# Loading the first weight products' operands by halves of their columns, and moving the rank rows of B behind four products

## The chip, the cores and the metric

The kernel runs on one NeuronCore of a Trainium2 chip. The metric is the device time of one execution in microseconds. A core has engines that run side by side, each with its own queue of instructions in order: TensorE (PE, matrix products), VectorE (DVE) and ScalarE (ACT) and GpSimd (POOL) for elementwise work, and SyncE (SP), which here only issues transfers from DRAM into SBUF, the memory on the chip. Products accumulate in banks of PSUM. Instructions of different engines wait for one another by semaphores.

## The reference

One block of a transformer on x (32 sequences of 64 tokens, 1024 features, float32):

```python
base  = einsum('bsi,oi->bso', x, W)                    # W: 1024 x 1024
low   = einsum('bsi,bir->bsr', x, lora_A[labels])      # rank 32
c     = base + einsum('bsr,or->bso', low, lora_B_w) * 0.5
qkv   = c @ w_qkv.T + b_qkv                            # 1024 q, 256 k, 256 v
...   # rotary positions, causal softmax attention, 32 heads over 8 key heads
x     = x + attention @ w_o.T + b_o
c2    = x @ W2.T + 2 * (rank-16 rows of two experts of eight)
x     = x + c2 @ W_base.T + b_base + 2 * (rank-16 rows of two experts of eight)
```

The kernel doesn't form c. It multiplies the weights first: W with w_qkv (called cq for the q columns and ckv for the rest), and W2 with W_base (cf). It keeps these products in DRAM (`cqkv`, `cffn`) and then applies them to x. The low-rank part goes the same way: the rows of `lora_B_w` times w_qkv are `b1q`, the "rank rows of B".

## The kernel before

**The weight products.** `multiply` (L514) forms a 1024 x 1024 product in four groups of two output blocks, each by a seven-product scheme (Strassen in Winograd's form; class `Group`, L220). Per group the left operand is a tile w of 256 outputs (128 partitions x 8 chunks x 256), of which `weight_sums` (L163) makes four sums s1 to s4 on GpSimd; the right operand is split by chunks (first and second H = 4 of 8) and by columns (first and second half), and `column_sums` (L176) makes four sums t1 to t4 of its quarters on VectorE. For cq the right operand is `wq`, 128 partitions x 8 chunks x 1024 columns. t1 (L182) is the second column half less the first, over the first four chunks; t2 (L184) takes t1 from the second column half of the last four chunks; t3 (L186) and t4 (L188) follow. One such sum is made per chunk, four each.

The seven steps of a group are p1 to p7 (L270 to L320). Each is four matrix products over the four chunks, eight instructions on TensorE, 128 x 512 outputs:

- p1 multiplies w's first four chunks, first 128 outputs, with wq's first four chunks, first column half. It fills bank x, tile cq_x in the profile.
- p2 adds to bank x the last four chunks of w, first 128 outputs, with wq's last four chunks, first column half.
- p6 multiplies s2 and t2 into bank y (cq_y); p5 multiplies s1 and t1 into bank z (cq_z); p7 adds s3 by t3 to bank y; p4 adds w's last quarter by t4 to bank y; p3 adds s4 by wq's last quarter to bank z. Between them VectorE and ScalarE read the banks, and ScalarE's queue writes the outputs to DRAM.

So p1 and p2 need one column half of wq and one output half of w alone; all the rest need sums over everything.

**The rank rows.** `rank_rows` (L473) multiplies b1 (1024 x 32 rows of B, 128 KB) with wq, four chunks at once in four stripes of 32 rows. It has two halves, `b1q_rows[0]` over wq's first four chunks and `b1q_rows[1]` over the last four, all columns, sixteen instructions each (tile b1q, L487). The second half copies two tiles on ScalarE and leaves a last step, two products `b1qs` (L480) that add the stripes, in the list `later`; `done_later` (L439) carries it out.

**The order.** TensorE's, VectorE's and SP's orders are written out by hand (`manual_schedule`, L120 to L125); GpSimd's and ScalarE's are left to a scheduler. For cq the first two groups are interleaved by the `order` list (L602): p1 of group 0, p1 of group 1, p2 of both, p6, p5, p7 of group 0, p6 of group 1, and so on. The dictionary `after` (L606) hangs other work behind a step: the first half of the rank rows behind (0, "p1"); `load_first` (L577) behind (0, "p2"), which carries out the second half of the rank rows and then issues the loads of x; `after_first_sum` (L589) behind (0, "p6"), which carries out `done_later`, makes t4, and prepares the gathers of `lora_A`.

**The loads.** SP issues them in the order of L551 to L560: w0 (group 0's w) first four chunks, wq's chunks 0 to 3 with b1 behind chunk 0, w1 first four chunks; then the same for the last four chunks; then `index` and the constants. Each chunk of wq is 512 KB in rows of 4 KB, and so is each half of w0 and w1. Eight loads of SP's queue are in flight at a time; the next one waits for the landing of the one eight before it. Group 2's w and then x wait for w0's last use, in (0, "p4").

Of the kernel before, what the change touches and what calls it, by code (L numbers as in the profile page):

```python
# [19 lines left out]
P = 128  # L20
D = 1024
KC = D // P
# [54 lines left out]
def block_kernel(ctx: ExitStack, tc: tile.TileContext, a, out: bass.AP):  # L77
    nc = tc.nc
# [33 lines left out]
    def load_x(hf):  # L112
        t = [xp.tile([P, TH], F32, tag=f"x{kc}", name=f"x{kc}_{hf}") for kc in range(KC)]
        for kc in range(KC):
            nc.sync.dma_start(t[kc], a["xT"][kc, :, hf * TH : (hf + 1) * TH])
        return t
# [17 lines left out]
    def labels_and_languages():  # L134

        nc.vector.tensor_copy(lab, index[:, :B])
        nc.vector.tensor_scalar(wrap, lab, 0.0, float(NL), ALU.is_lt, ALU.mult)
        nc.vector.tensor_add(lab, lab, wrap)
        nc.vector.tensor_scalar(lab, lab, 0.0, float(NL - 1), ALU.max, ALU.min)

        nc.vector.tensor_scalar(lab, lab, float(P), row, ALU.mult, ALU.add)
        nc.vector.tensor_copy(rows_of, lab)


        nc.vector.tensor_copy(lang, index[:, B:])
        nc.vector.tensor_scalar(lang, lang, float(E), None, ALU.subtract)
        nc.vector.tensor_tensor(
            lbias,
            em8.unsqueeze(1).to_broadcast([P, B // 2, E]),
            lang.unsqueeze(2).to_broadcast([P, B // 2, E]),  # L150
            ALU.is_equal,
        )
        nc.vector.tensor_scalar(lbias, lbias, 5.0, None, ALU.mult)
# [4 lines left out]
    H = KC // 2  # L158
# [274 lines left out]
    def new_low(hf):  # L433
        return hp.tile([P, TH], F32, tag="hw", name=f"low_{hf}")
# [4 lines left out]
    def done_later():  # L439
        while later:  # L440
            later.pop(0)()
# [15 lines left out]
    with tc.tile_pool(name="gen", bufs=1) as gen:  # L457
# [15 lines left out]
        def rank_rows(name, low, right, n, dst):  # L473


            banks = {at: ps_tile(f"{name}_{at}") for at in range(0, n, 512)}

            def stacked(at, rows):
                ps = ps_tile(f"{name}s_{at}")
                nc.tensor.matmul(ps, stack, rows, start=True, stop=True)  # L480
                nc.scalar.copy(dst[:, at : at + 512], ps)

            def half(i):
                for at, ps in banks.items():
                    for g in range(4):
                        kc = i * H + g
                        nc.tensor.matmul(  # L487
                            ps[g * LR : (g + 1) * LR], low[:, kc, :], right[:, kc, at : at + 512],
                            start=i == 0, stop=i == 1,
                        )  # L490
                    if i == 1:
                        rows = tmp(f"{name}o_{at}")
                        nc.scalar.copy(rows, ps)
                        later.append(lambda at=at, rows=rows: stacked(at, rows))

            return lambda: half(0), lambda: half(1)
# [48 lines left out]
        wq = gen.tile([P, KC, D], F32, tag="right", name="wq")  # L545
# [2 lines left out]
        w3x = gen.tile([P, KC, NF - D], F32, tag="w3x", name="w3x")  # L548
        b1 = gen.tile([P, KC, LR], F32, tag="b1", name="b1")
        w0, w1 = (wp.tile([P, KC, WG], F32, tag="w", name=f"w_cq{g}") for g in range(2))  # L550
        first_half, second_half = slice(0, H), slice(H, KC)  # L551
        for half in (first_half, second_half):
            nc.sync.dma_start(w0[:, half], a["w1"][0, :, half])
            for kc in range(half.start, half.stop):
                nc.sync.dma_start(wq[:, kc, :], a["wqkv"][:, kc, :D])
                if kc == 0:
                    nc.sync.dma_start(b1, a["b1"])
            nc.sync.dma_start(w1[:, half], a["w1"][1, :, half])
        nc.sync.dma_start(index, a["index"])
        nc.sync.dma_start(cst, a["consts"])  # L560
        b1q_rows = rank_rows("b1q", b1, wq, D, b1q)
# [9 lines left out]
        def gather_first(s):  # L571
            tags = iter(("w_os", "s_os"))
            first_pass[s] = gathered(
                0, s, lambda name: gen.tile([P, 4, KC * LR], F32, tag=next(tags), name=name), 4
            )

        def load_first(w):  # L577
            b1q_rows[1]()
            first_pass["x"], first_pass["low"] = load_x(0), new_low(0)

        def first_ranks(s):
            *halves_of_ranks, stacked = ranks(0, s, first_pass["x"], first_pass[s], first_pass["low"])
            for step in halves_of_ranks:
                step()
            later.append(stacked)
            if s == 0:
                gather_first(1)

        def after_first_sum(w):  # L589
            done_later()  # L590
            for kc in range(H):
                t_cq.make(kc, (3,))
            labels_and_languages()
            gather_first(0)

        def load_kv(w):
# [7 lines left out]
                *((0, "out11"), (0, "p4"), (0, "p3"), (1, "p5"), (1, "p7"), (1, "out11"), (1, "p4"), (1, "p3")),  # L604
            ],
            after={  # L606
                (0, "p1"): lambda w: b1q_rows[0](),
                (0, "p2"): load_first,
                (0, "p6"): after_first_sum,
                (1, "p3"): load_kv,  # L610
                (2, "p7"): lambda w: first_ranks(0),
                (2, "p4"): lambda w: done_later(),
# [137 lines left out]
    for hf in range(2):  # L750
# [264 lines left out]
        with tc.manual_schedule():  # L1015
# [3 lines left out]
            for u in range(2):  # L1019
                g = pair  # L1020
# [139 lines left out]
        w = wp.tile([P, KC, WG], F32, tag="w", name=f"w_h{hf}")  # L1160
# [165 lines left out]
```

## Time and profile before

| | us |
|---|---|
| median of 4 runs | 1227.49 (1226.78 to 1227.98) |
| profiled execution, its own time | 1226.07 |
| its span, first to last instruction | 1224.3 |
| TensorE busy | 1207.7 (99% of the span) |
| VectorE, GpSimd, ScalarE busy | 578.2, 512.2, 153.5 |
| first product starts | 7.27 |
| first landing of a load (half of w0) | 5.53 |
| landing of wq's chunk 4, and chunk 7 | 15.69, 19.55 |
| landing of w1's second half, the last of the weights | 20.81 |
| (0, "p6") starts, and the next product after it | 26.76, 30.20 |

The page gives busy times by engine, a chain of waits that ended last, and groups of instructions by line. Busy time of TensorE counts instructions that overlap as a pipeline, so 99% says that it is seldom without work, not that it runs at its peak. Idle time of another engine costs nothing as long as TensorE's chain doesn't pass through it. In rows that list instructions by time, the columns are start, length (both in us), engine, line, operation, what is written and read, and in brackets the idle time before and what ended it. "DMA" among the releasers is the landing of a load.

### The profile page before, as it was taken

Reading aid. Unit: us, or ns where it says so; the run is one execution under the profiler, and the core shown is the slowest. Engines: PE = TensorE matmul, PEld = TensorE weight load, DVE = VectorE, ACT = ScalarE, POOL = GpSimd, SP = SyncE. Lnnn points to the kernel's source line nnn. Section 1 sums busy time; section 2 is a strip of 40 time slices with the busy share of each in tenths; the row PEclk is TensorE's granted clock in tenths of the full one; section 3 lists DMA queues with packets and bytes.
Section 4 is the critical chain, followed back from the end, with each engine's and each line's share of the span. In section 5 each row is a group of like instructions: output and inputs, shape, how many; then the busy total and the mean of one; then the engine's idle time right before and its main releaser. Section 6 shows DMA issues by size and latency. Waiting matters only on the chain.

```text
span 1224.3 us, 13566 instructions
## 1 busy us (share of the span) xinstructions
PE 1207.7 (99%) x5434; PEld 610.8 (50%) x5434; DVE 578.2 (47%) x940; ACT 153.5 (13%) x282; POOL 512.2 (42%) x437
## 2 busy tenths in 40 slices
PE   7999999999999999999999999999999999999998
PEld 2444875555444477444444444444468444444443
DVE  4312141115557879753941113555879764743111
ACT  1001000000001124220000000001124330000000
POOL 3441361443434746843726111533646752822010
PEclk9999999999999999999999999999999999999999
DMA  6663732644111112023114234111111123212110
GB/s 240 211 212 108 270 123 82 206 148 146 35 34 35 36 70 70 17 67 126 35 35 138 69 122 153 35 35 35 35 70 33 39 70 98 76 35 69 48 56 35
DMA packets 57504, 108.83 MB, mean 89 GB/s; under 512 B 5088, under 2 KB 34144, under 8 KB 56160
## 3 DMA queue, kind: packets, MB, share of 16 engines
q1 hardware_dynamic: 41648, 79.53, 19.5%
q10 hardware_dynamic: 13104, 20.03, 4.5%
q0 software_dynamic: 2688, 8.39, 2.1%
q8 instruction: 43, 0.70, 0.3%
q14 instruction: 21, 0.17, 0.0%
HBM read 83.72 MB, written 24.22 MB: 88 GB/s over the span
## 4 chain that ended last, share of the span: by engine, by line
PE 94%; POOL 2%; DVE 2%; DMA 0%; issue 0%; ACT 0%; SPq 0%; POOLq 0%; DVEq 0%
PE qk_y L249 9%; PE f_y L249 7%; PE qk_x L249 6%; PE qk_z L249 6%; PE o_y L249 5%; PE v L843 5%; PE f_z L249 4%; PE f_x L249 4%; PE o_z L249 4%; PE o_x L249 4%; PE cq_y L249 3%; PE cf_y L249 3%; PE cq_x L249 2%; PE cq_z L249 2%; PE cf_x L249 2%; PE cf_z L249 2%
## 5 line engine op out<-in xcount | busy, mean ns | idle before, releaser
L793 POOL TENSOR_TENSOR raw<-raw,consts 128x512 f32<-128x512 f32 x40 | 65.4, 1646 | 99.8 <-DVE t L792 99.8
L897 POOL TENSOR_TENSOR e<-e,top 128x512 f32<-128x512 f32 x64 | 65.0, 1045 | 65.1 <-DVE top L896 50.1
L909 POOL TENSOR_TENSOR e<-e,tot 128x512 f32<-128x512 f32 x64 | 66.2, 1067 | 19.9 <-DVE tot L907 19.9
L249 PE MATMUL qk_x<-x,w_qk 128*128 128x512 f32 x160 | 72.9, 598 | 0.0
L249 PE MATMUL qk_y<-sum_x,s_qk 128*128 128x512 f32 x160 | 72.0, 593 | 0.0
L170 POOL TENSOR_TENSOR s_f<-w_f 128x512 f32<-128x512 f32 x8 | 11.2, 1403 | 121.1 <-DMA w_f<-cffn 99.6
L249 PE MATMUL o_x<-q,w_o 128*128 128x512 f32 x128 | 58.9, 592 | 0.0
L843 PE MATMUL v<-w_v,x 128*128 128x256 f32 x256 | 58.7, 382 | 0.0
L249 PE MATMUL f_x<-x,w_f 128*128 128x512 f32 x128 | 57.9, 592 | 0.0
L249 PE MATMUL f_y<-sum_y,s_f 128*128 128x512 f32 x128 | 57.5, 592 | 0.0
L906 DVE TENSOR_REDUCE tot<-e 128x8 f32<-128x512 f32 x64 | 40.2, 665 | 25.4 <-ACT e L901 25.1
L843 PEld LDWEIGHTS v<-w_v,x 128*128 128x128 f32 x256 | 47.4, 190 | 8.4 <-issue 2.6
L1001 POOL TENSOR_TENSOR x<-x,o_u 128x512 f32<-128x512 f32 x32 | 42.1, 1325 | 22.7 <-DVE o_u L291 18.4
L249 PEld LDWEIGHTS qk_x<-x,w_qk 128*128 128x128 f32 x160 | 29.6, 190 | 39.6 <-issue 39.6
L249 PEld LDWEIGHTS qk_y<-sum_x,s_qk 128*128 128x128 f32 x160 | 30.3, 190 | 37.9 <-issue 36.6
L170 POOL TENSOR_TENSOR s_qk<-w_qk 128x512 f32<-128x512 f32 x10 | 18.2, 1818 | 66.5 <-DMA w_qk<-cqkv 51.2
L794 DVE TENSOR_TENSOR t<-t,consts 128x512 f32<-128x512 f32 x40 | 45.0, 1137 | 1.0
L803 DVE TENSOR_TENSOR q<-raw,t 128x512 f32<-128x512 f32 x32 | 40.9, 1282 | 9.3 <-POOL raw L793 9.3
L901 ACT ACTIVATE e<-e 128x512 f32<-128x512 f32 x64 | 38.2, 640 | 47.4 <-POOL e L897 47.4
L887 DVE TENSOR_TENSOR e<-sc,consts 128x512 f32<-128x512 f32 x64 | 39.5, 679 | 8.1 <-PE sc L864 8.1
L249 PEld LDWEIGHTS f_x<-x,w_f 128*128 128x128 f32 x128 | 24.3, 190 | 30.6 <-issue 30.6
L249 PEld LDWEIGHTS f_y<-sum_y,s_f 128*128 128x128 f32 x128 | 24.3, 190 | 30.6 <-issue 30.6
(314 smaller groups left out, 2187.9 us busy)
## 6 DMA issues: line engine op xcount, KB each, us to landing
w_qk<-cqkv SPq DMA_DIRECT2D x10, 1024.0 KB, 5.6
x<-in_xT SPq DMA_DIRECT2D x16, 512.0 KB, 8.4
w_o<-in_wo SPq DMA_DIRECT2D x16, 512.0 KB, 4.8
s_o<-wos SPq DMA_DIRECT2D x16, 512.0 KB, 6.3
w_f<-cffn SPq DMA_DIRECT2D x8, 1024.0 KB, 5.6
outT<-o ACTq DMA_DIRECT2D x32, 256.0 KB, 2.4
wq<-in_wqkv SPq DMA_DIRECT2D x8, 512.0 KB, 9.0
cqkv<-cq ACTq DMA_DIRECT2D x16, 256.0 KB, 2.6
```

The lines of the kernel that those rows point to most:

```text
L170: nc.gpsimd.tensor_add(s[:, 0], a21, a22)
L249: nc.tensor.matmul(ps, self.weights[left][:, kc, :], self.right(right, kc), start=first and kc == 0, stop=kc == self.h - 1, skip_group_che ...
L793: nc.gpsimd.tensor_mul(rv, rv, c3)
L794: nc.vector.tensor_mul(t2v, t2v, s3)
L803: nc.vector.tensor_add(*unfinished.pop())
L843: nc.tensor.matmul(begun[t], x[kc][:, t * P : (t + 1) * P], wv[:, kc, :], start=False, stop=kc == KC - 1, skip_group_check=True,)
L887: nc.vector.tensor_add(per_key(e), per_key(sc), mask.unsqueeze(1).to_broadcast([P, 8, S]))
L897: nc.gpsimd.tensor_sub(ev, ev, wide(top))
L901: nc.scalar.activation(e, e, AF.Exp, scale=SCALE)
L906: nc.vector.tensor_reduce(tot[:, i], es[i], AX.X, ALU.add)
L909: nc.gpsimd.tensor_mul(es[i], es[i], wide(tot[:, i]))
L1001: nc.gpsimd.tensor_add(xo, xo, by_sequence(add))
```

## The change

The loads of w0, w1 and wq for the first weight products come in pieces. A chunk of wq is loaded in two halves of 512 columns, and a half of w0 or w1 in two pieces of 128 outputs. The pieces that p1 and p2 of the first two groups read go first: w0, wq and w1, first output half and first column half, for the first four chunks and then for the last four. Behind them come w0's second output half, b1, wq's second column half of chunks 0 to 3, w1's second output half, and wq's second column half of chunks 4 to 7. The bytes are the same. wq's rows in a load become 2 KB, those of w0 and w1 512 B; there are 25 loads in place of 13.

The first half of the rank rows moves from behind (0, "p1") to behind (1, "p2"), so that the four products p1, p1, p2, p2 run without it; the second half moves from `load_first`, behind (0, "p2"), to `after_first_sum`, behind (0, "p6"); and `done_later`, which stacks the stripes, moves from there to behind (0, "p3").

```diff
-        first_half, second_half = slice(0, H), slice(H, KC)
-        for half in (first_half, second_half):
-            nc.sync.dma_start(w0[:, half], a["w1"][0, :, half])
+
+        halves_of = slice(0, H), slice(H, KC)
+
+        def load_columns(kc, c):
+            cols = slice(c * D // 2, (c + 1) * D // 2)
+            nc.sync.dma_start(wq[:, kc, cols], a["wqkv"][:, kc, cols])
+
+        def load_outputs(w, g, half, r):
+            nc.sync.dma_start(w[:, half, r * P : (r + 1) * P], a["w1"][g, :, half, r * P : (r + 1) * P])
+
+        for half in halves_of:
+            load_outputs(w0, 0, half, 0)
             for kc in range(half.start, half.stop):
-                nc.sync.dma_start(wq[:, kc, :], a["wqkv"][:, kc, :D])
-                if kc == 0:
-                    nc.sync.dma_start(b1, a["b1"])
-            nc.sync.dma_start(w1[:, half], a["w1"][1, :, half])
+                load_columns(kc, 0)
+            load_outputs(w1, 1, half, 0)
+        for half in halves_of:
+            load_outputs(w0, 0, half, 1)
+        nc.sync.dma_start(b1, a["b1"])
+        for kc in range(H):
+            load_columns(kc, 1)
+        for half in halves_of:
+            load_outputs(w1, 1, half, 1)
+        for kc in range(H, KC):
+            load_columns(kc, 1)
         nc.sync.dma_start(index, a["index"])
         nc.sync.dma_start(cst, a["consts"])
...
         def load_first(w):
-            b1q_rows[1]()
             first_pass["x"], first_pass["low"] = load_x(0), new_low(0)
...
         def after_first_sum(w):
-            done_later()
+            b1q_rows[1]()
             for kc in range(H):
                 t_cq.make(kc, (3,))
...
             after={
-                (0, "p1"): lambda w: b1q_rows[0](),
                 (0, "p2"): load_first,
+                (1, "p2"): lambda w: b1q_rows[0](),
                 (0, "p6"): after_first_sum,
+                (0, "p3"): lambda w: done_later(),
```

## The prediction

> **What bounds the kernel now.** I read the page first, then the chain of waits for the stretch that the change touches (the first 62 us), then the order of time of VectorE, GpSimd and the DMA queue there, and last the transfer rates of loads with short rows.
>
> ```profile
> span 1224.3 us, 13566 instructions
> ...
> PE 1207.7 (99%) x5434; PEld 610.8 (50%) x5434; DVE 578.2 (47%) x940; ACT 153.5 (13%) x282; POOL 512.2 (42%) x437
> ...
> PE 94%; POOL 2%; DVE 2%; DMA 0%; issue 0%; ACT 0%; SPq 0%; POOLq 0%; DVEq 0%
> ```
>
> TensorE is the path nearly everywhere: 16.6 us of the span are not PE time, and 7.3 of them lie at the start. So the change can win only at the start, and loses what it adds there. The chain of waits for this stretch (start, length, what):
>
> ```profile
> 1.20 5.94 DMA wq<-in_wqkv
> ...
> 7.27 5.25 PE cq_x L249 x8
> 12.52 1.85 PE b1q L487 x16
> 14.38 7.06 PE cq_x L249 x16
> 21.44 1.85 PE b1q L487 x16
> 23.29 3.63 PE cq_x L249 x8
> 26.92 3.43 PE cq_y L249 x8
> 30.36 1.72 PE b1qs L480 x4
> ```
>
> The first product waits for the first 0.5 MB of weights w0 and the first 0.5 MB of wq, until 7.27. From there on TensorE waits for nothing: four products cq_x (p1, p1, p2, p2), the two halves of the rank rows b1q between them, and at 26.9 the first cq_y, p6. In order of time p6 begins at 26.76 and the next product at 30.20. A product of eight instructions takes 3.43 when its data are there. The first takes 5.25: its first four instructions start at 7.27, 8.26, 9.11 and 9.96, the last four 0.43 apart. wq's chunks 1 and 2 had landed by 8.78 and 10.05, so these starts are mostly a slower TensorE at its beginning, not data.
>
> p6 needs VectorE's second column sums (t2, L184), and these need the last columns of wq. VectorE and GpSimd in order of time:
>
> ```profile
> 15.79 1.75 DVE L184 TENSOR_TENSOR sum_cq<-wq,sum_cq 128x512 f32<-128x512 f32 x1 [7.93 <-DMA wq<-in_wqkv]
> 17.46 1.75 DVE L182 TENSOR_TENSOR sum_cq<-wq 128x512 f32<-128x512 f32 x1
> 20.81 0.68 DVE L182 TENSOR_TENSOR sum_cq<-wq 128x512 f32<-128x512 f32 x1
> 21.52 1.65 DVE L184 TENSOR_TENSOR sum_cq<-wq,sum_cq 128x512 f32<-128x512 f32 x1
> 24.88 1.64 DVE L184 TENSOR_TENSOR sum_cq<-wq,sum_cq 128x512 f32<-128x512 f32 x1
> ...
> 15.72 1.27 POOL L172 TENSOR_TENSOR s_cq<-w_cq 128x512 f32<-128x512 f32 x1
> 16.95 1.72 POOL L171 TENSOR_TENSOR s_cq<-s_cq,w_cq 128x512 f32<-128x512 f32 x1
> 20.88 1.75 POOL L170 TENSOR_TENSOR s_cq<-w_cq 128x512 f32<-128x512 f32 x1 [0.54 <-DMA w_cq<-in_w]
> ```
>
> Two readings. First, the same VectorE sum takes 0.68 while GpSimd waits for a load (20.81) and 1.65 to 1.75 while GpSimd adds weights; both engines then end one instruction every 1.67 (VectorE at 17.54, 19.2, 20.89): they take turns, 1.26 of GpSimd and about 0.4 of VectorE, and a sum ends 0.55 after the GpSimd instruction that it waited for. Second, the eighth sum ends at 26.52. p6 wants it only for its last chunk, 2.6 after its start at 26.76, so 2.8 of slack cover it. This slack, not TensorE's queue, is what the change spends.
>
> Rates, in a stretch of 4 KB rows and along two other loads (GB/s by fortieths of 58 to 74 us, wkv with 2 KB rows, and of 570 to 578 us, w_h with 512 B rows):
>
> ```profile
> 8.00:12.00 4.00, 4.00 (x8) 1.42 (x6) 0.00 (x0) 0.00 (x0) 0.00 (x0) 1.00 1.02 414
> ...
> GB/s 420 430 410 471 369 440 348 384 446 369 446 405 430 394 399 399 384 399 410 410 405 399 399 394 379 404 389 410 420 451 517 389 430 389 430 266 82 0 0 0
> ...
> GB/s 0 0 0 0 0 0 0 0 0 0 0 20 64 102 212 310 351 343 351 346 351 336 302 289 292 289 292 292 292 367 322 366 353 418 418 394 394 404 413 433
> ```
>
> With the queue full: 414 for 4 KB rows, about 400 for 2 KB, and 292 to 350 for 512 B; 292 is the level where rows of 512 B are cut from longer rows in DRAM, as the pieces of w0 and w1 will be.
>
> **The change, part by part.**
>
> *Start.* The first product needs 0.25 MB of w0 and 0.25 MB of wq in place of 0.5 and 0.5. Before, the first 0.5 MB were there at 5.53 (GpSimd starts on them at 5.60). So TensorE starts at about 5.8 in place of 7.27: 1.4 earlier. The bounds are 0.5 and 2: the first microseconds run at 120 to 290 GB/s, and short rows may be slower there. The four products then run without rank rows: 5.8 + 5.25 + 3 x 3.43 = 21.3, each half chunk of wq landing 0.66 after the one before and TensorE taking 0.86. The first half of the rank rows (1.85, same 16 instructions) ends at 23.2; its columns and b1 have landed by then. TensorE is ready for p6 at 23.2, 3.6 earlier than before. If data were there, the end would be 23.2 + 3.43 + 1.85 = 28.5 against 30.2 before.
>
> *Loads.* The same bytes in 25 loads in place of 13 (index and consts not counted). SP needs 0.47 an issue, under the 0.65 to 0.9 that 0.25 MB take, and its eight loads in flight hold over 5 us of work, so the issues hide. But the second half of wq's columns is now last. Up to the second half of wq's chunk 4 (the first that t2 needs) go 8 pieces of w (2.10 MB at 292: 7.2), 13 of wq (3.41 MB at 400: 8.5) and b1 (0.3): 16.0 us. Before, all 6.42 MB at 414 are 15.5 and landed at 20.8, so 5.3 go to the start, a slower stretch and the last receipt. That puts the landing, call it L, at 21.3. One thing is new in this window: the first output of cq (0.26 MB written, 0.65) leaves at about 18.6, while before it was issued at 22.09, behind all loads. L = 21.9; before, this chunk had landed at 15.7. Bounds: 20.0 if short rows go at the 350 of the same row (6.0 for w's pieces) and the write finds room, and 23 if the slow start hurts rows of 512 B by their number.
>
> A rule to weigh here: the Trainium skill, "DMA: Bandwidth & Descriptors", section Specifications, gives 512 B as the smallest transfer at line rate. The rows above don't bear that out (292 against 414). By the rule the loads up to there would take 13.6, L would be 19.5, and the sum below would come out 2.4 smaller, at no change.
>
> *VectorE.* Its order is unchanged: t1 and t2 of chunk 0, then 1, 2, 3. All after the first t1 sits behind L: seven sums, where before they began at 15.79. GpSimd's four sums for w0 start 6.3 before L and take 4 x 1.26 and a turn of VectorE, so its four for w1 begin 0.8 before L and stand in turns with VectorE: t2 of chunk 0 ends at L + 0.95, then at 1.67 each t1, t2 of chunk 1 and t1 of chunk 2 (L + 5.96), then three alone at 0.65: L + 7.9 = 29.8. Bounds: L + 5 without turns (7 x 0.68), L + 8.7 if one turn more falls in.
>
> *p6 and the rank rows.* p6's last chunk starts at 29.85 and the next product at 30.75, where it was 30.20: +0.55. Before, both halves of the rank rows lay ahead of this point; now the second half lies behind it, on the path: +1.85. The stacking b1qs (1.72) moves from here to behind (0, p3) and is paid once in both.
>
> *What is moved past what.* p5 now waits behind the rank rows; its t1 and s1 are long there. t3 (2.48) runs after t2 and ends at 32.3, p7 begins at about 36. The labels, rows_of and GpSimd's gathers shift with it by under 3 us; After the gathers GpSimd waited 6.36 for its next weights. index and consts land some 3 us later; they are wanted at 33 and, for b1qs, at about 51. The next weights w2 and x go out when (0, p4) is done, which moves with TensorE. The copies of b1qo on ScalarE and its two temporary tiles live 18 us longer among eleven. I cost all of these at nothing; if that cover fails, a wait of one instruction (0.6 to 1.2) is the size. The wait of 0.84 at 56.95 remains.
>
> **Sum.** 0.55 + 1.85 = +2.4. Against the profiled execution: span 1224.3, time 1226.07, so 1228.5; the median of the runs is 1227.49, 1.4 above the profiled one, and 2.4 on it gives 1229.9. From the bounds of L, -1.9 and +1.1, and of VectorE's stretch, -2.9 and +0.8.
>
> **The rivals.**
> 1. *The sums come in time; not slower.* One mechanism, in the loads: short rows come in faster than I take them. It decides from L = 19.5 on, where 0.55 + 1.85 are just made up (21.9 - 2.4): 1227.5. For it: the 350 GB/s in the same row, with which w's pieces take 6.0, and L is 20.7 with the write and 20.0 where the write finds room. Against it: the 292 behind it. Even so it hardly gains, since VectorE still has its turns.
> 2. *TensorE alone sets the end.* GpSimd leaves VectorE alone and L is at 19: the end is 28.5, 1.7 less: 1225.8. Against it: every sum beside a GpSimd sum took 1.6 or more.
> 3. *TensorE slows down again.* In p6 it waits between chunks for some 3 us in all; if it then runs at the pace of its beginning (0.85 for 0.43) for about four instructions, 1.7 come on top: 1231.6. For it: that slow beginning. Against it: the wait of 0.84 at 56.95, after which one instruction was late by 0.1 only. The Trainium skill, "TensorE: Matmul & The Clock Gate", Part 1, says that it takes an idle window of about 3.4 us to slow the array; none of the single waits here reaches that.
> 4. *The landing is later still* (the queue of short rows, the slow start): L = 23, +3.5: 1231.0.
>
> **How the numbers follow.** 0.2% is 2.45 us, about what a measurement of this kernel can tell from no change; the likeliest sum lies at this border. The main case (VectorE's sums behind L gate p6) has 0.62, half of it above the border; rival 1 has 0.13 and rival 2 0.05, of which 0.04 would show as faster; rivals 3 and 4 have 0.10 each. Slower 0.52, same 0.44, faster 0.04. The range reaches from L at 20.0 (+0.5: 1228.0), which leaves out most of rivals 1 and 2, to rival 3 (1231.6) and a little over it for a landing that is late as well: 1232.0.
>
> **What would show it.** In the new profile: the first product at about 5.8; the four cq_x without b1q between; p6's instructions apart, each pair released by VectorE's t2 (sum_cq), with its last at about 30; VectorE's sums at 1.65 from about 22 on; GB/s under 350 where w's pieces load; b1q after p6. Wrong would be: p6 without gaps (rivals 1 and 2), or instructions of 0.85 apart behind it (rival 3), or waits of TensorE after 62 us that were not there.

## The result and the profile after

The changed kernel takes 1228.65 us (median of 32 runs, 1227.41 to 1233.37) against 1227.4 us (52 runs, 1225.99 to 1228.55). The ratio is 1.0013, with a 95% interval of 1.0008 to 1.0017: slower by 1.0 to 2.1 us, inside the forecast range and under the border of 0.2%. The medians differ by 1.25. The profiled execution took 1228.19 us with a span of 1226.4 (before 1226.07 and 1224.3).

The page's head and chain of the changed kernel:

```profile
span 1226.4 us, 13588 instructions
...
PE 1209.0 (99%) x5434; PEld 611.2 (50%) x5434; DVE 576.1 (47%) x940; ACT 153.5 (13%) x282; POOL 510.6 (42%) x437
...
PE 93%; POOL 2%; DVE 2%; DMA 1%; issue 1%; SPq 0%; ACT 0%; POOLq 0%; DVEq 0%
```

The totals hardly tell anything: TensorE has a share of 93% of the chain in place of 94, DMA has 1. The first 32 us tell it. TensorE in order of time:

```profile
4.87 16.20 PE L249 MATMUL cq_x<-wq,w_cq 128*128 128x512 f32 x32 [4.87 <-DMA wq<-in_wqkv]
21.00 1.92 PE L487 MATMUL b1q<-wq,b 128*32 128x512 f32 x16
22.86 1.13 PE L249 MATMUL cq_y<-sum_cq,s_cq 128*128 128x512 f32 x2
25.45 1.13 PE L249 MATMUL cq_y<-sum_cq,s_cq 128*128 128x512 f32 x2 [1.47 <-DVE sum_cq L184]
27.85 1.12 PE L249 MATMUL cq_y<-sum_cq,s_cq 128*128 128x512 f32 x2 [1.27 <-DVE sum_cq L184]
29.18 1.13 PE L249 MATMUL cq_y<-sum_cq,s_cq 128*128 128x512 f32 x2 [0.20 <-DVE sum_cq L184]
30.23 1.93 PE L487 MATMUL b1q<-wq,b 128*32 128x512 f32 x16
32.09 3.70 PE L249 MATMUL cq_z<-sum_cq,s_cq 128*128 128x512 f32 x8
```

The first product starts 2.4 us earlier, and TensorE is ready for p6 at 22.86, 3.9 earlier than before. Then p6, one line before, falls into four pairs, the last three behind a wait for VectorE's t2 (L184). It ends at 30.23, where it ended at 30.20 before, and only then come the second half of the rank rows. The next product starts at 32.09, that is 1.89 behind its place before. VectorE, and below it GpSimd with the four sums for w1:

```profile
21.11 0.94 DVE L184 TENSOR_TENSOR sum_cq<-wq,sum_cq 128x512 f32<-128x512 f32 x1 [3.31 <-DMA wq<-in_wqkv]
21.97 1.76 DVE L182 TENSOR_TENSOR sum_cq<-wq 128x512 f32<-128x512 f32 x1
23.77 1.63 DVE L184 TENSOR_TENSOR sum_cq<-wq,sum_cq 128x512 f32<-128x512 f32 x1
25.32 1.75 DVE L182 TENSOR_TENSOR sum_cq<-wq 128x512 f32<-128x512 f32 x1
27.10 0.69 DVE L184 TENSOR_TENSOR sum_cq<-wq,sum_cq 128x512 f32<-128x512 f32 x1
...
28.43 0.69 DVE L184 TENSOR_TENSOR sum_cq<-wq,sum_cq 128x512 f32<-128x512 f32 x1
```

```profile
20.23 1.27 POOL L172 TENSOR_TENSOR s_cq<-w_cq 128x512 f32<-128x512 f32 x1
21.46 1.72 POOL L170 TENSOR_TENSOR s_cq<-w_cq 128x512 f32<-128x512 f32 x1
23.26 1.59 POOL L171 TENSOR_TENSOR s_cq<-s_cq,w_cq 128x512 f32<-128x512 f32 x1
24.93 1.59 POOL L173 TENSOR_TENSOR s_cq<-w_cq,s_cq 128x512 f32<-128x512 f32 x1
```

VectorE's first t2 waits for the landing of chunk 4's second columns (21.02 in the trace; the whole chunk was there at 15.69 before). The next three sums take 1.63 to 1.76 beside GpSimd, whose sums end at 26.52; the last three take 0.68 to 0.69. The transfer rates over the first 26 us, in fortieths (0.65 us each):

```profile
GB/s 0 0 13 236 260 288 353 372 292 296 297 258 230 347 357 388 388 347 323 295 295 329 372 384 384 370 324 293 318 353 360 375 391 315 167 303 25 84 116 367
```

The stretches near 292 are the 512 B pieces of w0 and w1. Behind 32 us the distance stays: the first ckv product starts at 119.03 before and at 121.03 after.

### The profile page after: what moved, and what is told of

Its sections match the earlier page's. It is cut to its first block, busy times and chain, and to the rows that moved or that the text cites. A ratio compares the mean times of both kernels' runs of the same rounds, so it can differ in the third digit from the quotient of the medians.

```text
span 1226.4 us, 13588 instructions
## 1 busy us (share of the span) xinstructions
PE 1209.0 (99%) x5434; PEld 611.2 (50%) x5434; DVE 576.1 (47%) x940; ACT 153.5 (13%) x282; POOL 510.6 (42%) x437
## 4 chain that ended last, share of the span: by engine, by line
PE 93%; POOL 2%; DVE 2%; DMA 1%; issue 1%; SPq 0%; ACT 0%; POOLq 0%; DVEq 0%
PE qk_y L249 9%; PE f_y L249 7%; PE qk_x L249 6%; PE qk_z L249 6%; PE o_y L249 5%; PE v L859 5%; PE f_z L249 4%; PE f_x L249 4%; PE o_z L249 4%; PE o_x L249 4%; PE cf_y L249 3%; PE cq_y L249 3%; PE cq_z L249 2%; PE cf_z L249 2%; PE cf_x L249 2%; PE sc L880 2%
```

## The experiments

They ran on three chips, each with runs of the kernel before on the same chip, and every ratio is to those. The stages are compared by one mark: when the product behind p6 and the rank rows starts (for before 30.20, where p6 ends; its b1qs, which comes there, stands elsewhere in the others). Times of the mark and of landings are from each run's trace, of one execution.

The granted clock is the share of TensorE's full clock that the profile records; its record begins when the full clock is granted for the first time. Until then instructions of 128 x 512 start 0.85 apart, behind it 0.43 (6.71, 7.56, 8.41 and then 10.18, 10.61 in the changed kernel, where it comes at 9.37).

**First chip (before: 1233.47, 35 runs).** Here all kernels are some 6 us slower, before as well. All four profiles of this chip have two waits of TensorE that no profile of the other chips has, far from the change: 1.1 us at 656 to 659, and 2.3 us (3.7 in e5) ahead of a product at 661 to 664. In e1 and e5 a half clock follows. These are 3.4 us and more of the 6; what causes them was not followed. The changed kernel itself did not run on this chip, so the runs of this chip are compared with before alone.

*e1: the loads of before, the rank rows' places of after.* From the kernel before:

```diff
         def load_first(w):
-            b1q_rows[1]()
...
         def after_first_sum(w):
-            done_later()
+            b1q_rows[1]()
...
-                (0, "p1"): lambda w: b1q_rows[0](),
                 (0, "p2"): load_first,
+                (1, "p2"): lambda w: b1q_rows[0](),
                 (0, "p6"): after_first_sum,
+                (0, "p3"): lambda w: done_later(),
```

> The loads of before with the order of the rank rows of after. Theory (the late column sums cost, the order alone does not): TensorE starts at 7.3, the four products end at 22.9, the first half of the rank rows at 24.7, p6 runs without waits since t2 ends at 26.5 as before, the product after the second half of the rank rows starts at about 30.0 (30.20 before, 32.09 after). No change against before, -0.5 to +0.3 us, none of the slower executions with a lower clock. Rival (the order of the rank rows itself costs, by later copies or the later stacking): +1 to +2 us as after.

Measured: ratio 0.9998 (0.9986 to 1.0010). p6 runs in one piece (26.24 to 29.87), t2 ends at 26.32. The mark is at 31.72 and not at 30.0, as the four products took 16.96 in place of 15.6: in this execution the full clock of TensorE was granted at 13.27 only, at 10.45 in the profile before. By the times the order alone costs nothing that can be measured; their interval is -1.7 to +1.2 us, so the lower end of the rival's +1 to +2 is not excluded by them. The profile speaks against it: behind the four products there is no wait up to the mark.

*e2: the loads of after, both halves of the rank rows ahead of p6.* This edit and the next two are to the changed kernel:

```diff
         def after_first_sum(w):
-            b1q_rows[1]()
...
-                (1, "p2"): lambda w: b1q_rows[0](),
+                (1, "p2"): lambda w: [b1q_rows[i]() for i in range(2)],
```

> The loads of after, but both halves of the rank rows behind the four products, ahead of p6. Theory: TensorE waits in p6 anyway until about 29.2 for the last chunk of t2, and the second half of the rank rows fits into this wait; the product after p6 starts at 30.1 to 30.3, against 32.09 after and 30.20 before: -0.3 to +0.3 us against before. Rival (something behind p6, or the transfers of x and w2, costs the time): +1 to +2 us, as after.

Measured: ratio 0.9985 (0.9973 to 0.9997); 0.0015 of 1233.47 are 1.85 us less than before (0.4 to 3.3), more than either theory gave. The mark is at 29.36, 0.84 ahead of before; where the rest comes from was not followed. t2 ends at 28.34, so p6 still hangs on VectorE, but the 1.85 of the rank rows is gone from the path.

*e3: GpSimd's sums for w1 only behind t3.*

```diff
+        mark = gen.tile([P, 1], F32, tag="mark", name="mark")
+        t3_made = nc.gpsimd.tensor_copy(mark, t_cq.tiles[2][H - 1][:, :1])
...
+                    with tc.issue_after(t3_made.ins) if (name, g) == ("cq", 1) else ExitStack():
-                    s = weight_sums(ws[g], f"{name}{g}")
+                        s = weight_sums(ws[g], f"{name}{g}")
```

> As after, but GpSimd makes w1's four sums only when VectorE has made t3 (one copy of 128 x 1 on GpSimd reads t3 and stands before them). Theory (VectorE and GpSimd take turns): VectorE's sums after the landing at 21.0 take 0.7 each, t2 ends at 25.7 in place of 29.1, p6 waits little and ends at 26.6, the product behind the second half of the rank rows starts at 28.5 (32.09 after): -1.3 to -2.0 us against before. Rival (the landings alone set the end of t2): t2 still ends at 28 to 29 and the time stays at +1 to +2 us.

Measured: ratio 0.9976 (0.9964 to 0.9988), about -3.0 us (-1.5 to -4.4), more than the -1.3 to -2.0 expected; the mark gives -1.40. VectorE in e3:

```profile
21.15 0.69 DVE L184 TENSOR_TENSOR sum_cq<-wq,sum_cq 128x512 f32<-128x512 f32 x1 [3.31 <-DMA wq<-in_wqkv]
21.76 0.68 DVE L182 TENSOR_TENSOR sum_cq<-wq 128x512 f32<-128x512 f32 x1
22.48 0.69 DVE L184 TENSOR_TENSOR sum_cq<-wq,sum_cq 128x512 f32<-128x512 f32 x1
...
25.14 0.69 DVE L184 TENSOR_TENSOR sum_cq<-wq,sum_cq 128x512 f32<-128x512 f32 x1
```

The same landing (VectorE starts at 21.15, 21.11 after), and every sum takes 0.69. t2 ends at 25.83 in place of 29.12, the mark is at 28.80 in place of 32.09. The turns cost 3.3 us of the path, by the mark of after and e3; the landings don't hold t2 at 29. GpSimd's sums for w1 now stand beside VectorE's t4 (6.52 for its four sums in place of 2.49), for which TensorE doesn't wait.

*e5: wq by column halves, w0 and w1 in whole rows.*

```diff
-        def load_outputs(w, g, half, r):
-            nc.sync.dma_start(w[:, half, r * P : (r + 1) * P], a["w1"][g, :, half, r * P : (r + 1) * P])
-
-        for half in halves_of:
-            load_outputs(w0, 0, half, 0)
+        def load_half(w, g, half):
+            nc.sync.dma_start(w[:, half], a["w1"][g, :, half])
+
+        def load_group(half):
+            load_half(w0, 0, half)
             for kc in range(half.start, half.stop):
                 load_columns(kc, 0)
-            load_outputs(w1, 1, half, 0)
+            load_half(w1, 1, half)
+
         for half in halves_of:
-            load_outputs(w0, 0, half, 1)
+            load_group(half)
         nc.sync.dma_start(b1, a["b1"])
-        for kc in range(H):
-            load_columns(kc, 1)
-        for half in halves_of:
-            load_outputs(w1, 1, half, 1)
-        for kc in range(H, KC):
+        for kc in range(KC):
             load_columns(kc, 1)
```

> As after, but w0 and w1 come in halves of whole 4 KB rows as before; only wq comes by column halves. Theory (the 512 B rows make the landings late and put w1's sums beside VectorE's): the first product starts at 6.2 (4.87 after), wq's chunk 4 is there at 18.9 to 19.3 (21.0 after), w1's sums on GpSimd end at about 21.5, t2 ends at about 25, and the product after the second half of the rank rows starts at 28.9 (32.09 after): -0.9 to -1.5 us against before. Rival (2 KB rows of wq and the order of its halves are what is late): t2 ends past 28 and the time stays above before.

Measured: ratio 0.9984 (0.9970 to 0.9999), about -2.0 us. VectorE's first t2 and p6 in e5:

```profile
18.84 0.72 DVE L184 TENSOR_TENSOR sum_cq<-wq,sum_cq 128x512 f32<-128x512 f32 x1 [0.95 <-DMA wq<-in_wqkv]
...
25.08 3.70 PE L249 MATMUL cq_y<-sum_cq,s_cq 128*128 128x512 f32 x8
```

GpSimd's w1 sums end at 20.68, t2 at 24.61, and p6 runs in one piece. So the column halves of wq are not what is late. The bytes ahead of chunk 4's second columns are the same as in the changed kernel, and their earlier landing (VectorE starts on them at 18.84 in place of 21.11) goes to the longer rows of w, with 21 loads in place of 25. That GpSimd is out of VectorE's way has a second cause: in whole rows w1's second output half comes along with the first, ahead of wq's second columns. The run doesn't tell the shares of the two. The mark was missed, 30.56 for 28.9: the four products took 16.68, with the full clock at 12.15. So with data in time TensorE's slow beginning is on the path, and it has another length in each execution.

**Second chip (before: 1227.37, 25 runs).**

*c0: the changed kernel again.* No edit.

> The changed kernel once more, as the measure for the other runs of this chip. Theory: TensorE waits in p6 for t2, so the pace of its first instructions (slow for 3 to 6 us, another length in each execution) doesn't reach the end here, while before it does by half. Then before has the larger spread over executions at the same chip, and the difference of the medians is below the 1.9 us that the two first profiles showed at the product after p6: +0.5 to +1.6 us against before. Rival (the change costs the same in every execution): +1.9 us, like spreads.

Measured: 1229.21, ratio 1.0012 (1.0003 to 1.0021). The spread is no smaller than that of before (the middle half of the executions spans 1.85 us against 1.05), against the theory, and the profile shows one source of it. TensorE in c0, then busy times by stretch (length, PE, PEld, DVE, ACT, POOL, granted clock, DMA):

```profile
25.42 1.13 PE L249 MATMUL cq_y<-sum_cq,s_cq 128*128 128x512 f32 x2 [0.50 <-DVE sum_cq L184]
27.82 3.45 PE L249 MATMUL cq_y<-sum_cq,s_cq 128*128 128x512 f32 x4 [1.27 <-DVE sum_cq L184]
31.20 2.09 PE L487 MATMUL b1q<-wq,b 128*32 128x512 f32 x16
```

```profile
24.00:28.19 4.19, 2.42 (x5) 0.70 (x5) 4.16 (x4) 0.00 (x0) 2.41 (x2) 1.00 0.37 117
28.19:31.60 3.41, 3.41 (x8) 0.76 (x10) 3.38 (x7) 0.00 (x0) 0.00 (x0) 0.50 0.00 0
```

From 28.19 to 31.60 the granted clock is 0.50. The last two chunks of p6 end at 31.20 in place of 30.23, and the mark is at 33.23 in place of 32.09, though t2 ends at 29.09 as after. This is rival 3 of the prediction, in one of the profiles.

The traces of all runs say when it comes. In every one of the fourteen profiles the granted clock changes at whole multiples of 3.4133 us behind the moment at which the full clock began: here 28.19 is 11.12 + 5 x 3.4133, in e1 665.22 is 13.27 + 191 x 3.4133. Laid on this grid, the stretch ahead of the drop in c0 has TensorE at work for 1.65 us:

```profile
24.78:28.19 3.41, 1.65 (x4) 0.60 (x4) 3.38 (x4) 0.00 (x0) 1.63 (x2) 1.00 0.36 116
```

It is 1.26 in e1 and nothing in e5. In the changed kernel's profile the grid cuts the same waits of p6 into stretches with 1.94 and 1.94 us of work, in c1 with 2.17 and 1.95, and no drop follows. No stretch with 1.78 us (the least, in e2) or more is followed by a half clock in any profile; each with 1.65 or less is. So in c0 the waits of p6 in sum caused the drop, and whether they do depends on where the grid falls.

Over all runs of the changed kernel a mean clock of 0.998 or less, the sign of such a stretch, came in 5 of 34 executions on the first measuring, 3 of 11 here and 2 of 11 on the third chip; for before in 0 of 25 here and 0 of 32 there. It is a rough sign: every profile ends at half clock for a varying time, which moves the mean too (0.999 for before). On the first chip it can't be used, as 25 of 35 executions of before have it as well.

*e4: e2 and e3 together.* Both diffs above.

> Both of the earlier edits on the kernel after: both halves of the rank rows ahead of p6, and w1's sums on GpSimd only after t3. Theory: t2 ends at 25.7, TensorE is then the bound, the product after p6 starts at 27.9 to 28.2 (29.36 with the first edit alone, 28.80 with the second alone): 0.6 to 0.9 us below the second alone, -1.8 to -2.5 us against before. Rival (the landing of wq's last chunk at 23 to 23.6 holds the second half of the rank rows, so nothing is left to gain): 28.8 as with the second edit alone.

Measured: 1224.76, ratio 0.9976 (0.9966 to 0.9986), -2.6 us by the medians. TensorE goes without a wait from 20.62 to beyond the mark, which is at 27.72 against 28.80 for e3. The landing doesn't hold the rank rows.

*e7: before, with three zero products ahead.* Added to the kernel before:

```diff
+        warm = tmp("warm")
+        nc.vector.memset(warm, 0.0)
+        warm_bank = ps_tile("warm_bank")
+        for i in range(3):
+            nc.tensor.matmul(warm_bank, warm[:, :P], warm, start=i == 0, stop=i == 2)
```

> The kernel of before with three products of a zero tile on TensorE ahead of all else, done before the first load has landed; their sum is never read. Theory (TensorE's slow start lies on the path of before): the first cq_x product takes 3.4 in place of 5.25, the product after p6 starts at 28.4 to 28.6 (30.20 before), -1.5 to -2.5 us against before, and the executions spread less. Rival (the slow start is data, not TensorE): the first product still takes 5 and nothing changes.

Measured: 1227.01, ratio 0.9994 (0.9985 to 1.0003), no change. TensorE in e7:

```profile
1.47 5.34 PE L549 MATMUL warm_bank<-warm 128*128 128x512 f32 x6 [1.47 <-DVE warm L546]
7.34 1.10 PE L249 MATMUL cq_x<-wq,w_cq 128*128 128x512 f32 x2 [0.53 <-DMA wq<-in_wqkv]
8.94 2.40 PE L249 MATMUL cq_x<-wq,w_cq 128*128 128x512 f32 x4 [0.50 <-DMA wq<-in_wqkv]
11.50 1.12 PE L249 MATMUL cq_x<-wq,w_cq 128*128 128x512 f32 x2 [0.16 <-DMA wq<-in_wqkv]
12.55 1.92 PE L487 MATMUL b1q<-wq,b 128*32 128x512 f32 x16
```

The full clock is there before the first product (6.53), and that product ends at 12.55 all the same (12.45 before): it waits for a chunk of wq every 1.3 us. The rival holds: the first product of before is bound by its data, and the slow clock hides behind them. The eleven runs of e7 lie between 1226.14 and 1227.41, the 25 of before between 1225.81 and 1230.16; that the longer ones of before are those with a long slow stretch would fit, but no profile shows it.

*e8: an early small piece, the rest of w in whole rows, rank rows first, two zero products.* Two zero products and the rank rows as above, in the changed kernel; the loads:

```diff
-        def load_outputs(w, g, half, r):
-            nc.sync.dma_start(w[:, half, r * P : (r + 1) * P], a["w1"][g, :, half, r * P : (r + 1) * P])
-
-        for half in halves_of:
-            load_outputs(w0, 0, half, 0)
-            for kc in range(half.start, half.stop):
-                load_columns(kc, 0)
-            load_outputs(w1, 1, half, 0)
-        for half in halves_of:
-            load_outputs(w0, 0, half, 1)
+        def load_outputs(w, g, half, rs):
+            nc.sync.dma_start(w[:, half, rs], a["w1"][g, :, half, rs])
+
+        first, second, both = slice(0, P), slice(P, WG), slice(0, WG)
+        load_outputs(w0, 0, halves_of[0], first)
+        for kc in range(H):
+            load_columns(kc, 0)
+        load_outputs(w1, 1, halves_of[0], both)
+        load_outputs(w0, 0, halves_of[0], second)
+        load_outputs(w0, 0, halves_of[1], both)
+        for kc in range(H, KC):
+            load_columns(kc, 0)
+        load_outputs(w1, 1, halves_of[1], both)
         nc.sync.dma_start(b1, a["b1"])
-        for kc in range(H):
-            load_columns(kc, 1)
-        for half in halves_of:
-            load_outputs(w1, 1, half, 1)
-        for kc in range(H, KC):
+        for kc in range(KC):
             load_columns(kc, 1)
```

> One small first piece of w0 and wq by column halves as after, the rest of w0 and w1 in whole rows; both halves of the rank rows ahead of p6; two zero products ahead of all else. Theory: first product at 4.9, the four products end at 19.1, the rank rows at 22.8 to 23, t2 at 24.6 to 25.4, and the product after p6 starts at 26.3 to 26.6: -3.5 to -4.5 us against before. Rival (w1's sums stand beside VectorE's again, or the landings of wq's last columns are at 23): the product after p6 at 28 or later, -2 us.

Measured: 1223.14, ratio 0.9961 (0.9947 to 0.9975), -4.2 us by the medians, from five executions: it beats both kernels. TensorE in e8:

```profile
5.04 3.92 PE L249 MATMUL cq_x<-wq,w_cq 128*128 128x512 f32 x8
9.74 10.57 PE L249 MATMUL cq_x<-wq,w_cq 128*128 128x512 f32 x24 [0.78 <-DMA w_cq<-in_w]
20.24 3.64 PE L487 MATMUL b1q<-wq,b 128*32 128x512 f32 x32
23.81 3.70 PE L249 MATMUL cq_y<-sum_cq,s_cq 128*128 128x512 f32 x8
27.35 3.60 PE L249 MATMUL cq_z<-sum_cq,s_cq 128*128 128x512 f32 x8
```

The mark is at 27.35, 0.75 behind the end of what was expected, as the second product waited for w1's first half until 9.70. GpSimd had finished its sums at 21.52, t2 ended at 25.45, and p6 never waited. By the mark the gain is 2.85, by the spans of the two profiles 3.4; the rest of the 4.2 lies between the profiled executions and the medians and was not followed.

**Third chip (before: 1227.43, 32 runs).**

*c1: the changed kernel once more.*

> The changed kernel as the measure for the three other runs of this chip: +0.5 to +2 us against before, and in some of its executions a granted clock of 0.997 or 0.998 where before has 0.999 or 1.000.

Measured: 1228.90, ratio 1.0011 (1.0002 to 1.0020). Its profile has the mark at 31.59, with t2 ending at 28.62 and no drop of the clock; two of eleven executions have 0.997 and 0.998.

*e10: products in the waits of p6.* Added to the changed kernel:

```diff
+    filler = psum.tile([P, 512], F32, tag="ps", name="filler")[:, :256]
...
+                if (self.name, left) == ("cq0", "s2") and kc < 2:
+                    for i in range(3):
+                        nc.tensor.matmul(
+                            filler, self.weights["11"][:, i, :], self.right("11", i)[:, :256],
+                            start=kc == i == 0, stop=kc == 1 and i == 2,
+                        )
```

> As after, with three products of 128 x 256 behind each of the first two chunks of p6, in the waits; their sum is never read. Theory (the waits in p6 leave TensorE idle for so much of 3.4 us that its clock is halved for a stretch in some executions): p6 ends where it did, at 30.2, no execution has a clock of 0.998 or less, the slow tail is gone and the median is 0.3 to 1.0 us below the changed kernel. Rival (the drops have nothing to do with p6): as many drops as in the changed kernel, and the same time or up to 0.5 us more.

Measured: 1228.62, ratio 1.0010 (1.0001 to 1.0019), 0.3 below c1, which the intervals don't separate. No execution of eleven has a clock under 0.999. At the rate of c0 and c1 (5 of 22) eleven in a row without a drop would come in about 6 of 100 tries, so the runs alone point to the waits in p6 as the cause and don't settle it; the grid of c0 above does for the one drop that was profiled. One execution (1230.26) was as long as a tail run of c1 without a low clock, so the tail may have another source too.

*e2 again.* The edit of e2.

> The earlier run with both halves of the rank rows ahead of p6, once more on this chip. Theory: the second half of the rank rows costs 1.85 us where the change puts it and nothing in TensorE's wait; it also fills that wait, so the clock holds: 1.8 to 2.5 us below the changed kernel, -0.8 to +0.3 us against before. Rival (it is the landing alone): no more than 0.5 us below the changed kernel.

Measured: 1226.27, ratio 0.9989 (0.9980 to 0.9998), 2.6 below c1. TensorE in this run:

```profile
22.00 3.64 PE L487 MATMUL b1q<-wq,b 128*32 128x512 f32 x32
25.57 3.23 PE L249 MATMUL cq_y<-sum_cq,s_cq 128*128 128x512 f32 x6
29.00 1.13 PE L249 MATMUL cq_y<-sum_cq,s_cq 128*128 128x512 f32 x2 [0.20 <-DVE sum_cq L184]
29.97 3.60 PE L249 MATMUL cq_z<-sum_cq,s_cq 128*128 128x512 f32 x8
```

From the end of t2 to the mark it takes 1.02 (28.95 to 29.97), in c1 2.97 (28.62 to 31.59): 1.95 for the second half of the rank rows. No clock under 0.999.

*e9: e8 without the zero products.* No other edit.

> The kernel with the early piece, without its two zero products. If the zero products matter (theory): the first instructions are slow for 3.4 to 6.8 us from 4.9 on, p1 of group 0 ends 0.5 to 1.5 us later, -2.0 to -3.5 us against before. If the first products are bound by their data as in before (rival): the same as with the zero products, -3.5 to -4.5 us against before.

Measured: 1224.27, ratio 0.9972 (0.9962 to 0.9981), -3.2 us. The four products take 16.66 (15.20 in e8), with the full clock granted at 10.53 (5.68 in e8), and the mark is at 28.74 against 27.35. Once the data come early, the slow beginning is on the path, and two zero products take 1.4 us off by the marks, 1.0 by the two differences to before, which are from two chips; the intervals of the two ratios overlap, so the profiles and not the times decide between theory and rival.

## Why the prediction was right, and where it was off

**The mechanism is shown.** p6 waits chunk by chunk for t2 (the new profile), e3 takes the turns away and t2 ends 3.3 earlier with the landing unchanged, and in e5, with w in whole rows, the landing comes 2.3 earlier and p6's waits vanish. The second term, the rank rows behind p6, measures 1.86 in the profile and 1.95 between e2 and c1 (forecast 1.85). On the third chip this alone decides: with the rank rows ahead of p6 (e2) the kernel is 2.6 us below the changed one, and the two intervals don't touch. The sum was 2.4; the profile has 1.89 at the mark, the runs 1.0 to 2.1.

**A mis-sized term of the sum is the landing L.** "L = 21.9" came out at 21.02. From 9 us on the pieces took about what I gave them (0.84 to 0.90 for w, 0.66 to 0.73 for wq between the trace's landings). The 0.65 of cq's first output was put at the wrong place: it is issued at 18.30, and the trace shows a longer interval only before chunk 7 (22.34 to 23.63), which t2 reaches later than it lands. VectorE's stretch behind L was right: L + 7.9 forecast, 8.1 measured. So p6's end moved by 0.03 in place of 0.55.

**The step from the profile to the median** was off by more. I took the 1.4 us by which before's median lies above its profiled execution over to the changed kernel, where it is 0.46. The profiled executions differ by 2.12, close to the sum; the medians only by 1.25, so that 1228.65 came out where I had 1229.9. Why the offset is smaller was not followed. The result lies 0.65 above the low end of the range, an end that I had reasoned from an earlier landing (L at 20.0); that this miss stayed inside is luck.

**A wrong reading that cost nothing in the sum.** "These starts are mostly a slower TensorE at its beginning, not data" is half of it. The starts up to 9.96 are those of the slow clock, but e7 shows that without it the first product of before would end no earlier. The profile before had it already, in TensorE's weight loads:

```profile
8.82 0.63 PEld L249 LDWEIGHTS cq_x<-wq,w_cq 128*128 128x128 f32 x2 [1.08 <-DMA wq<-in_wqkv]
...
10.09 0.28 PEld L249 LDWEIGHTS cq_x<-wq,w_cq 128*128 128x128 f32 x1 [0.64 <-DMA wq<-in_wqkv]
...
11.38 0.32 PEld L249 LDWEIGHTS cq_x<-wq,w_cq 128*128 128x128 f32 x2 [0.54 <-DMA wq<-in_wqkv]
```

Each pair's weights waited for its chunk. I carried the 5.25 over to the new kernel, where the four products took 16.13 against my 15.5, with 2.9 us of waits in p6 behind them.

**The start** was 2.4 earlier, over the 1.4 given and past the bound of 2; it couldn't reach the end. The first 0.25 MB of w0 in 512 B rows landed at 4.07.

**The weighed rules.** The 512 B rows did load at about 292 GB/s, against the 414 of 4 KB rows before, so the line rate that the Trainium skill ("DMA: Bandwidth & Descriptors", Specifications) gives from 512 B on was not reached here. And rival 3, which I held against "TensorE: Matmul & The Clock Gate", Part 1, occurs: c0 shows it with single waits of 0.50 and 1.27 us, where the rule asks for an idle window of about 3.4. What failed in my reading is that I held single waits against the 3.4: in these traces the work in a stretch of 3.41 us counts, 1.65 in c0. The drop is not the cause of the slowdown, which the profiles without it show as well, but it lengthens the tail: the four longest of the first 34 executions, 1231.27 to 1233.37, all have a mean clock of 0.997 or 0.998.

**Rivals 1 and 2** fell: the loads were not fast enough, and GpSimd did not leave VectorE alone. Rival 4 (L at 23) did not come. The chances put half on the far side of the border of 0.2%; the outcome lies on the near side, at 0.13%.

## What to carry to other kernels

Splitting a load so that the first product can start earlier moves the last-needed piece to the end; ask what was hidden behind the old order of landing (here VectorE's sums) before counting the earlier start. Work that an engine can do while it waits for a late operand belongs ahead of that wait, not behind it: the same sixteen products cost 1.9 us on one side of p6 and nothing on the other. Keep rows long in all pieces but the first, bring early what another engine has to prepare (here w1's whole rows), and keep another engine's elementwise work out of the stretch in which two engines share the path.

## What the hardware showed

- The clock was halved for 3.41 us after a stretch of 3.41 us in which TensorE was at work for 1.65, with no single wait over 1.3 us (c0). In all fourteen profiles it changed only on a grid of 3.413 us that starts with the first full clock; stretches of the grid with 1.65 us of work or less were followed by half clock, those with 1.78 or more were not. In other executions of the same program it held.
- The moment at which TensorE's full clock is granted at the start varies for alike programs: 8.80, 9.37 and 11.12 in three profiles of the changed kernel, with the first product at 4.9 to 5.0. Three zero products of 128 x 512 from 1.47 on brought it to 6.53 (e7).
- VectorE and GpSimd, both adding pairs of SBUF operands, end one instruction each in 1.67 us (before and after); alone a VectorE sum takes 0.69 (e3) and a GpSimd sum 1.26.
